# Two-layer cross-attention on one NeuronCore: the softmax factors 1/l of layer 0 taken to the features by a VectorE transpose and a trip through DRAM, in place of TensorE transposes

## The chip, the cores and the metric

The kernel runs on one NeuronCore of a Trainium2 chip. The metric is device time in microseconds (us) of one execution; lower is better. The engines named below are TensorE (PE, with its weight loads as PEld), VectorE (DVE), ScalarE (ACT), GpSimd (POOL) and SyncE (SP, which only issues DMAs here).

## What is computed

Four batches of 1024 query rows of 512 features pass through two cross-attention layers, each with a residual. Everything is float32. The change lies in layer 0:

```python
# layer 0: 16 heads of 64, 1024 queries, 1024 keys
h = layernorm(x) * gamma + beta
Q = (h @ Wq).reshape(B, NQ, 16, 64)
K = (context @ Wk).reshape(B, NC, 16, 64)
V = (context @ Wv).reshape(B, NC, 16, 64)
attn = softmax(einsum("bihd,bjhd->bhij", Q, K), axis=-1) * 64 ** -0.5
x = x + einsum("bhij,bjhd->bihd", attn, V).reshape(B, NQ, 1024) @ Wo + bo
# layer 1: RMS norm, 16 heads of 32, rotary embedding, q and k of unit length
x = x + attention1(x, context) @ wout
```

The softmax divides by a row sum l, one for each query and head. The kernel multiplies by 1/l after the product with V, where the queries lie along the free dimension and the 128 partitions are the features of two heads. So each 1/l, which is made with queries on partitions, has to be turned and repeated over the 64 features of its head.

## The kernel before, in words

The 16 heads of layer 0 are done as 8 pairs (`p`), and the 1024 queries of a pair as 8 tiles of 128 (`i`). One call of `Attention0.step` (L381 and on) does one tile for both heads. Two steps, an even one and an odd one, make a block (`BQ = 2`); there are 32 blocks in a batch and 128 in all. A step runs so:

- `scores`: TensorE makes the scores of the two heads, 8 matmuls (L372).
- VectorE takes the row maximum (L393), and ScalarE the exponentials with their row sums, into `e` and `l` (L394), once for each head.
- Filler work on TensorE, taken from the list `work` by `Units.fill`: projections of the next pairs, output projection of earlier ones, in pieces with a cost in us, spread by a planner over the steps that are left.
- VectorE transposes `e` in 32x32 blocks (L399). After the odd step, 16 DMAs from SP's queue (L406) put these blocks in the order that a matmul wants, into `eT`: 128 KB and 128 runs of 1 KB each.
- VectorE takes the reciprocal of the sums (L410). In an even step with two blocks in hand, `product` multiplies the older one's `eT` by V (L451, 32 matmuls, "AV" from here on) and scales by the factors (L458). So AV of a block comes more than one step after its `eT` DMAs are issued.

The factors go a way of their own. In the even step, `factors` lets GpSimd spread the 4 sums' reciprocals of the block over 256 columns times 64 ** -0.5 (L424). At the top of the next even step, `factors_turned` has TensorE transpose them, two transposes of 128x128 (L442), right behind the scores; ScalarE copies the result from PSUM to the place where `vals` will stand (L443); and VectorE multiplies AV by that copy (L458).

What sets the order: the engines run their instructions in program order (`manual_schedule`), SP's queue holds the `eT` DMAs, the pairs' weights (L313), the rows of x (L287), and the stores. ScalarE's queue issues DMAs only at the very start. The framework gives every DMA, of SP's queue or of ScalarE's, one of eight completion semaphores in turn, in the order in which its scheduler wrote the program, and lets a DMA wait until the DMA eight places before it has landed. In the order written for this kernel, the even step's second exponential is over after the second or third `eT` DMA of the block before it (103 of 127 blocks), and the odd step's after the eighth or ninth (99 of 127).

Buffers: `e` has two, so that the exponentials of a block wait for the `eT` DMAs of the block two before. Four PSUM banks (`bank`) are used in turn by filler, transposes and AV.

Of the kernel before, what the change touches and what calls it, by code (L numbers as in the profile page):

```python
# [30 lines left out]
F32 = mybir.dt.float32  # L31
AF = mybir.ActivationFunctionType
ALU = mybir.AluOpType
AX = mybir.AxisListType

P = 128
# [7 lines left out]
HD0 = 64  # L44
# [63 lines left out]
def xattn_kernel(ctx: ExitStack, tc: tile.TileContext, a: dict, out: bass.AP):  # L108
    nc = tc.nc
# [3 lines left out]
    const = ctx.enter_context(tc.tile_pool(name="const", bufs=1))  # L113
    sb = ctx.enter_context(tc.tile_pool(name="sb", bufs=2))
    ps_s = ctx.enter_context(tc.tile_pool(name="ps_s", bufs=2, space=bass.MemoryType.PSUM))
    ps_f = ctx.enter_context(tc.tile_pool(name="ps_f", bufs=1, space=bass.MemoryType.PSUM))
    ctx.enter_context(tc.manual_schedule())

    def score(name, shape=(P, S)):
# [4 lines left out]
    def bank(name):  # L124

        which["n"] = which["n"] + 1 if which["n"] < 3 else which["from"]
        return ps_f.tile([P, 512], F32, tag=f"f{which['n']}", name=name)
# [5 lines left out]
    ident = const.tile([P, P], F32, name="ident")  # L133
# [2 lines left out]
    nc.gpsimd.memset(ones, 1.0)  # L136
    nhalf = const.tile([P, 16], F32, name="nhalf")
    nc.gpsimd.memset(nhalf, -0.5)
    cols = const.tile([P, 3, NQ], F32, name="cols")
    bo = const.tile([P, DQ], F32, name="bo")  # L140
    cos = const.tile([P, NT, HD1], F32, name="cos")
# [27 lines left out]
    def flush():  # L169
        while posts:  # L170
            posts.pop(0)()
# [120 lines left out]
    def add_units(xt, lhs, w, name, cs, then=None):  # L292

        n = len(cs)

        def one(t, i, pp=[None]):
            if i == 0:
                pp[0] = bank(f"{name}_{t}")
            matmul(pp[0], lhs(cs[i])[:, t * P : (t + 1) * P], w(cs[i]), i == 0, i == n - 1)
            if i == n - 1:  # L300
                nc.vector.tensor_add(xt[t], xt[t], pp[0])  # L301
                if then is not None:
                    then(t)

        return [[(0.86, lambda t=t, i=i: one(t, i)) for i in range(n)] for t in range(NT)]
# [51 lines left out]
    BQ = 2  # L357
    r = [slice(j * HD0, (j + 1) * HD0) for j in range(2)]

    class Attention0:  # L360
# [20 lines left out]
        def step(self, p, i, pr, us):  # L381
            n = f"{self.b}_{p}_{i}"
            sc = self.scores(p, i, pr)
            if i % BQ == 0 and len(self.blocks) == 2:
                self.factors_turned()
            m = sb.tile([P, 2], F32, tag="m", bufs=3, name=f"m_{n}")
            l = sb.tile([P, 2], F32, tag="l", bufs=3, name=f"l_{n}")
            if i % BQ == 0:
                self.e = sb.tile([P, BQ, 2, S], F32, tag="e", bufs=2, name=f"e0_{n}")
                self.li = sb.tile([P, BQ, 2], F32, tag="li", bufs=4, name=f"li_{n}")  # L390
            e = [self.e[:, i % BQ, j, :] for j in range(2)]
            for j in range(2):
                nc.vector.tensor_reduce(m[:, j : j + 1], sc[j], AX.X, ALU.max, negate=True)  # L393
                nc.scalar.activation(e[j], sc[j], AF.Exp, bias=m[:, j : j + 1], accum_out=l[:, j : j + 1])  # L394
            holds["posts"] = True
            self.u.fill(min(us, 1.8))
            holds["posts"] = False
            for j in range(2):
                nc.vector.transpose(e[j], e[j])  # L399
            flush()  # L400
            if i % BQ == BQ - 1:
                eT = sb.tile([P, 2 * BQ, 4, S // 4], F32, tag="big", bufs=2, name=f"eT_{n}")
                of = self.e.rearrange("p t h s -> p (t h) s")
                for g in range(4):
                    for q in range(4):
                        nc.sync.dma_start(  # L406
                            eT[32 * g : 32 * (g + 1), :, q, :],
                            of[32 * q : 32 * (q + 1), :, g * (S // 4) : (g + 1) * (S // 4)],
                        )
            nc.vector.reciprocal(self.li[:, i % BQ, :], l)  # L410
            if i % BQ == BQ - 1:
                eT = eT.rearrange("p (t h) a s -> p h t a s", h=2)
                self.blocks.append((p, i // BQ, pr, eT, self.li))
            elif self.blocks:
                if len(self.blocks) == 2:
                    self.product()
                self.factors()
            self.u.fill(us - min(us, 1.8))

        def factors(self):  # L420

            li = self.blocks[0][4]
            self.rb = sb.tile([P, BQ, P], F32, tag="rb", bufs=2, name=f"rb_{self.blocks[0][:2]}")
            nc.gpsimd.tensor_scalar(  # L424
                self.rb.rearrange("p t (j d) -> p (t j) d", j=2),
                li.rearrange("p t j -> p (t j)").unsqueeze(2).to_broadcast([P, 2 * BQ, HD0]),
                HD0**-0.5,
                0.0,
                ALU.mult,
                ALU.add,  # L430
            )

        def factors_turned(self):

            p, q, pr = self.blocks[0][:3]
            W = BQ * P
            if q == 0:
                pr["vals"] = sb.tile([P, S], F32, tag="vals", bufs=4, name=f"vals0_{self.b}_{p}")
            self.o = pr["vals"][:, q * W : (q + 1) * W]
            rT = bank(f"rT_{self.b}_{p}_{q}")  # L440
            for k in range(BQ):
                nc.tensor.transpose(rT[:, k * P : (k + 1) * P], self.rb[:, k, :], ident)  # L442
            nc.scalar.copy(self.o, rT[:, :W])  # L443

        def product(self):
            p, q, pr, eT, _ = self.blocks.popleft()
            o, W = self.o, BQ * P
            av = bank(f"av_{self.b}_{p}_{q}")
            for k in range(NT):
                for j in range(2):  # L450
                    nc.tensor.matmul(  # L451
                        av[r[j], :W].rearrange("p (t a i) -> p t a i", t=BQ, a=4),
                        pr["v"][:, k, r[j]],
                        eT[:, j, :, :, k * 32 : (k + 1) * 32],
                        start=k == 0,
                        stop=k == NT - 1,
                    )
            nc.vector.tensor_mul(o, av[:, :W], o)  # L458


    TH = 2
# [206 lines left out]
    def flat(lists):  # L668
        return [u for lst in lists for u in lst]
# [54 lines left out]
    work = Units()  # L724
# [7 lines left out]
    AV = 3.9  # L732
# [8 lines left out]
    for b in range(B):  # L741
        ct, hT, pairs = st["ct"], st["hT"], st["pairs"]
        xt = []
        att = Attention0(b, work)
# [3 lines left out]
        for p in range(NPAIR):  # L748
# [15 lines left out]
            elif p % 2 == 0:  # L764
                i = p // 2 - 1
                wo[i] = wo_load(a["Wo"], i, f"wo0_{b}_{i}")
                outs = add_units(
                    xt,
                    lambda n: pairs[n]["vals"],
                    lambda n, i=i: wo[i][:, n % 2, :],  # L770
                    f"po0_{b}_{i}",
                    (p - 2, p - 1),
                )
# [3 lines left out]
            if p == 6:  # L777
                kT, qT = qk_tile(f"k1_{b}_0"), qk_tile(f"q1_{b}_0")
                k = rotated_chains(kT, ct, NC_, lambda k, wk=wk: wk[:, k, :], f"k1_{b}_0", RowScratch())
                other = k[0][0] + outs[0] + k[1][0] + outs[1] + k[0][2] + outs[2] + k[2][0] + k[1][2] + outs[3]  # L780
            if p == NPAIR - 1:
                last = outs[4:]
                wo[3] = wo_load(a["Wo"], 3, f"wo0_{b}_3")
                outs = add_units(
                    xt, lambda n: pairs[n]["vals"], lambda n: wo[3][:, n % 2, :], f"po0_{b}_3", (6, 7)
                )
                xnT = []
                norms = norm_units(b, 1, xnT, lambda h: xt[4 * h : 4 * h + 4])
# [11 lines left out]
            for i in range(NT):  # L800
# [8 lines left out]
                n = NT * (NPAIR - p if later else 1) - i  # L809
# [15 lines left out]
        q = rotated_chains(qT, xnT, NQ, lambda k, wq=wq: wq[0][:, k, :], f"q1_{b}_0", tmp)  # L825
        k1 = rotated_chains(kT1, ct, NC_, lambda k, wk1=wk1: wk1[0][:, k, :], f"k1_{b}_1", tmp)
        q1 = rotated_chains(qT1, xnT, NQ, lambda k: wq1[:, k, :], f"q1_{b}_1", tmp)

        def second():
            att.product()  # L830
            att.factors()

        att.factors_turned()
        work.add([(AV, second)] + flat(outs[:4]) + norms[0]["stats"])
        work.add(k1[0][0] + [(0.2, att.factors_turned)] + norms[0]["apply"] + [(AV, att.product)])
        work.add(norms[0]["turn"] + q[0][0] + k1[1][0] + k1[0][2] + flat(outs[4:]) + q[0][2])
        work.drain()

# [2 lines left out]
        o = [  # L841
            sb.tile([P, S], F32, tag="vals", bufs=4, name=f"o1_{b}_{g}") if g < 2 else None
            for g in range(4)
        ]
# [6 lines left out]
        for half in range(2):  # L851
            n = 0
# [51 lines left out]
        else:  # L904
            outs = add_units(
                xt, lambda n, o=o: o[n], lambda n, w=wo1[1]: w[:, n % 2, :], f"po1_{b}_1", (2, 3), store
            )
# [39 lines left out]
```

## Time and profile before

| | |
|---|---|
| median of 3 runs | 2992.65 us (2991.08 to 2992.93) |
| the profiled execution: its time, its span | 2989.95 us, 2987.7 us |
| PE busy | 2917.3 us, 98% of the span |
| DVE busy | 2230.7 us, 75% |
| ACT busy | 1429.5 us, 48% |
| POOL busy | 416.6 us, 14% |
| DMA engines, mean share in layer 0 (four stretches of 460 to 480 us) | 0.72 to 0.73 |
| DMA engines, mean share in layer 1 | 0.03 to 0.09 |

Durations come from the one profiled execution, whose span runs from the first to the last instruction. TensorE's granted clock is 0.996 of full speed over the whole. Matmuls are pipelined, so a matmul's own duration is longer than its distance to the next; the times below that say what a matmul costs are distances from start to start. A wait is put down to what ended it last by the profile. Times in a timeline are us from the span's start.

### The profile page before, as it was taken

How to read it: one execution, taken by the hardware profiler on the slowest of the kernel's cores; microseconds unless marked ns; L12 is line 12 of the kernel's file. 1: busy time of each engine (PE TensorE's matmuls, PEld its weight loads, DVE VectorE, ACT ScalarE, POOL GpSimd, SP SyncE). 2: the span in 40 equal slices, each digit the busy share in tenths (PEclk: the TensorE clock that was granted, in tenths of full speed). 3: DMA queues.
4: the chain of work that ended last, by engine and by line, in shares of the span. 5: the costliest groups of instructions: out<-in, count | busy, mean ns of one | idle time of the engine just before them, and what ended most of it. 6: DMA issues, size and time to landing. Idle time of an engine off the chain costs nothing.

```text
span 2987.7 us, 60793 instructions
## 1 busy us (share of the span) xinstructions
PE 2917.3 (98%) x24748; PEld 1544.2 (52%) x24748; DVE 2230.7 (75%) x2824; ACT 1429.5 (48%) x2265; POOL 416.6 (14%) x392
## 2 busy tenths in 40 slices
PE   8999999999999999999999999999999999999998
PEld 5544546555544555655554454555455445455544
DVE  4777795877777779587777777958777777795777
ACT  3444443666443444465644344446664444444664
POOL 0010022420000002232000000223200000022310
PEclk9999999999999999999999999999999999999999
DMA  5788674010387867301048776730104978772000
GB/s 148 169 192 180 158 178 112 22 35 25 81 203 185 186 163 171 94 21 35 25 98 207 175 183 166 171 84 21 35 25 113 205 176 182 170 169 69 2 2 30
DMA packets 374134, 348.50 MB, mean 117 GB/s; under 512 B 37600, under 2 KB 355296, under 8 KB 373856
## 3 DMA queue, kind: packets, MB, share of 16 engines
q1 hardware_dynamic: 371664, 343.43, 48.4%
q8 instruction: 197, 3.23, 0.5%
q10 hardware_dynamic: 2192, 1.19, 0.2%
q14 instruction: 81, 0.66, 0.1%
HBM read 67.64 MB, written 8.39 MB: 25 GB/s over the span
## 4 chain that ended last, share of the span: by engine, by line
PE 78%; DVE 10%; DMA 4%; SPq 3%; ACT 2%; issue 1%; POOL 1%; DVEq 0%; ACTq 0%
PE s L372 14%; PE av L451 13%; PE po L158 10%; PE pv L158 7%; PE s L599 7%; PE av L638 6%; PE pqT L158 6%; PE pkT L158 5%; PE q_p L158 3%; DMA eT<-e 2%; SPq L406 2%; PE av L649 2%; DVE both L615 2%; DVE e L399 2%; PE k_p L158 1%; DVE m L393 1%
## 5 line engine op out<-in xcount | busy, mean ns | idle before, releaser
L394 ACT ACTIVATE e<-s,m 128x1024 f32<-128x1024 f32 x512 | 565.6, 1109 | 679.2 <-DVE m L393 613.8
L393 DVE TENSOR_REDUCE m<-s 128x1 f32<-128x1024 f32 x512 | 602.8, 1219 | 320.0 <-PE s L372 320.0
L399 DVE STREAM_TRANSPOSE e<-e 128x1024 f32<-128x1024 f32 x512 | 606.7, 1224 | 54.9 <-ACT e L394 43.0
L609 ACT ACTIVATE e<-s 128x1024 f32<-128x1024 f32 x512 | 496.5, 1022 | 315.1 <-PE s L599 300.1
L372 PE MATMUL s<-qk 64*128 64x512 f32 x2048 | 520.5, 615 | 6.0 <-ACT e L394 5.3
L451 PE MATMUL av<-eT,v 128*64 128x256 f32 x4096 | 474.8, 385 | 15.6 <-DMA eT<-e 13.7
L615 DVE TENSOR_TENSOR both<-e 128x512 f32<-128x512 f32 x512 | 342.4, 701 | 127.7 <-ACT e L609 92.5
L451 PEld LDWEIGHTS av<-eT,v 128*64 128x64 f32 x4096 | 289.4, 138 | 214.0 <-issue 53.7
L372 PEld LDWEIGHTS s<-qk 64*128 64x128 f32 x2048 | 181.8, 186 | 262.6 <-issue 188.9
L599 PE MATMUL s<-q,k 32*128 32x256 f32 x4096 | 305.7, 402 | 5.8 <-ACT q L526 2.7
L599 PEld LDWEIGHTS s<-q,k 32*128 32x128 f32 x4096 | 191.6, 185 | 149.7 <-ACT e L609 71.4
L158 PE MATMUL po<-wo,vals 128*128 128x512 f32 x512 | 239.6, 601 | 2.5 <-ACT v L130 2.5
L158 PE MATMUL pqT<-hT,w 128*128 128x512 f32 (+1 forms) x800 | 241.3, 597 | 0.7 <-ACT hT L255 0.7
L443 ACT COPY vals<-rT 128x256 f32<-128x256 f32 x128 | 47.7, 372 | 327.4 <-PE rT L442 327.4
L301 DVE TENSOR_TENSOR x<-x,po 128x512 f32<-128x512 f32 x200 | 133.8, 679 | 82.8 <-PE po L158 82.8
L158 PEld LDWEIGHTS pv<-w,cT 128*128 128x128 f32 (+1 forms) x2400 | 176.7, 152 | 30.3 <-issue 27.2
L158 PE MATMUL pv<-w,cT 128*128 128x128 f32 (+1 forms) x2400 | 186.5, 275 | 0.0
L158 PE MATMUL pkT<-cT,w 128*128 128x512 f32 (+1 forms) x600 | 181.6, 599 | 1.1 <-ACT cT L130 1.1
L619 DVE TENSOR_TENSOR both<-both 128x1024 f32<-128x1024 f32 x128 | 159.7, 1248 | 4.4
L158 PEld LDWEIGHTS po<-wo,vals 128*128 128x128 f32 x512 | 90.9, 190 | 106.4 <-issue 101.4
L158 PEld LDWEIGHTS pqT<-hT,w 128*128 128x128 f32 (+1 forms) x800 | 85.9, 151 | 112.2 <-issue 105.9
L638 PE MATMUL av<-e,v 128*32 128x256 f32 x2048 | 137.0, 385 | 0.0
(461 smaller groups left out, 2667.0 us busy)
## 6 DMA issues: line engine op xcount, KB each, us to landing
eT<-e SPq DMA_DIRECT2D x2048, 128.0 KB, 2.8
xr<-in_x_dram SPq DMA_DIRECT2D x32, 256.0 KB, 4.3
x<-in_x_dram SPq DMA_DIRECT2D x32, 256.0 KB, 3.8
wo<-in_Wo_dram SPq DMA_DIRECT2D x16, 512.0 KB, 4.2
out_dram<-x SPq DMA_DIRECT2D x32, 256.0 KB, 2.7
w<-in_Wq_dram SPq DMA_DIRECT2D x31, 256.0 KB, 4.0
c<-in_ctx_dram SPq DMA_DIRECT2D x32, 192.0 KB, 4.5
wkv<-in_wkv_dram SPq DMA_DIRECT2D x16, 384.0 KB, 3.5
```

The lines of the kernel that those rows point to most:

```text
L158: nc.tensor.matmul(o[rr], lhsT[:, rr], rhs, start=start, stop=stop)
L301: nc.vector.tensor_add(xt[t], xt[t], pp[0])
L372: nc.tensor.matmul(sc[j][:, kb * 512 : (kb + 1) * 512], pr["qT"][r[j], i * P : (i + 1) * P], pr["kT"][r[j], kb * 512 : (kb + 1) * 512], st ...
L393: nc.vector.tensor_reduce(m[:, j : j + 1], sc[j], AX.X, ALU.max, negate=True)
L394: nc.scalar.activation(e[j], sc[j], AF.Exp, bias=m[:, j : j + 1], accum_out=l[:, j : j + 1])
L399: nc.vector.transpose(e[j], e[j])
L451: nc.tensor.matmul(av[r[j], :W].rearrange("p (t a i) -> p t a i", t=BQ, a=4), pr["v"][:, k, r[j]], eT[:, j, :, :, k * 32 : (k + 1) * 32], ...
L599: nc.tensor.matmul(sc[j // 2][:, j % 2, c, :], kT[rr, g, k * P : (k + 1) * P], qT[rr, g, qb * WQ : (qb + 1) * WQ], start=True, stop=True,)
L609: nc.scalar.activation(e, sc[u], AF.Exp, scale=float(np.sqrt(np.float32(HD1))))
L615: nc.vector.tensor_add(self.both[:, kk, 2 * u : 2 * u + 2, :], es[u][:, :, 0, :], es[u][:, :, 1, :])
L619: nc.vector.tensor_add(self.both[:, 0], self.both[:, 0], self.both[:, kk])
L638: nc.tensor.matmul(self.av[rr, 0, :], v[g][:, 2 * kk + c, rr], es[j // 2][:, j % 2, c, :], start=first and c == 0, stop=end and c == 1,)
```

## The change

The reciprocals of a block are taken at once, after its odd step, into the first 4 columns of a 128x32 tile `sums` that is otherwise one. VectorE transposes that tile in 32x32 blocks into `turned`, so that the 128 queries of factor k lie on the 4 partitions k, k+32, k+64, k+96. In the next (even) step, behind the exponentials, ScalarE's queue issues 4 DMAs, one for each factor, of 4 runs of 128 B, to a DRAM tile `rows` (`factors_out`). In the odd step, again behind the exponentials, it issues 2 DMAs, one for each head, that read 256 numbers from DRAM back onto 64 partitions each, into `fac` (`factors_back`); they wait for the 4 to have landed. `product` then multiplies AV by 64 ** -0.5 and by `fac` in one VectorE instruction. The transposes, the PSUM bank they took, ScalarE's copy and GpSimd's spreading are gone. At the end of a batch the same calls stand in the list of work.

```diff
+    dram = ctx.enter_context(tc.tile_pool(name="dram", bufs=3, space=bass.MemoryType.DRAM))
+    sums = const.tile([P, 32], F32, name="sums")
+    nc.gpsimd.memset(sums, 1.0)
...
         def step(self, p, i, pr, us):
             sc = self.scores(p, i, pr)
-            if i % BQ == 0 and len(self.blocks) == 2:
-                self.factors_turned()
...
-                nc.scalar.activation(e[j], sc[j], AF.Exp, bias=m[:, j : j + 1], accum_out=l[:, j : j + 1])
+                l = self.l[:, i % BQ, j : j + 1]
+                nc.scalar.activation(e[j], sc[j], AF.Exp, bias=m[:, j : j + 1], accum_out=l)
+            if self.blocks:
+                (self.factors_back if i % BQ else self.factors_out)()
...
-            nc.vector.reciprocal(self.li[:, i % BQ, :], l)
-            if i % BQ == BQ - 1:
+                self.factors(n)
...
-            elif self.blocks:
-                if len(self.blocks) == 2:
-                    self.product()
-                self.factors()
+            elif len(self.blocks) == 2:
+                self.product()
+        def factors(self, n):
+            nc.vector.reciprocal(sums[:, : 2 * BQ].rearrange("p (j t) -> p t j", j=2), self.l)
+            turned = sb.tile([P, 32], F32, tag="li", bufs=1, name=f"li_{n}")
+            nc.vector.transpose(turned, sums)
+            self.turned = turned
+
+        def factors_out(self):
+            block = self.blocks[-1]
+            rows = dram.tile([2 * BQ, 4, 32], F32, tag="rows", name=f"rows_{block[0]}_{block[1]}")
+            for k in range(2 * BQ):
+                nc.scalar.dma_start(rows[k], self.turned[k : k + 97 : 32, :])
+            block[4] = rows.rearrange("(j t) a i -> j (t a i)", j=2)
+
+        def factors_back(self):
+            block = self.blocks[-1]
+            fac = sb.tile([P, BQ * P], F32, tag="rb", bufs=2, name=f"fac_{block[0]}_{block[1]}")
+            for j in range(2):
+                nc.scalar.dma_start(fac[r[j]], block[4][j].partition_broadcast(HD0))
+            block[4] = fac
...
-            rT = bank(f"rT_{self.b}_{p}_{q}")
-            for k in range(BQ):
-                nc.tensor.transpose(rT[:, k * P : (k + 1) * P], self.rb[:, k, :], ident)
-            nc.scalar.copy(self.o, rT[:, :W])
...
-            nc.vector.tensor_mul(o, av[:, :W], o)
+            nc.vector.scalar_tensor_tensor(o, av[:, :W], HD0**-0.5, fac, ALU.mult, ALU.mult)
...
-        att.factors_turned()
-        work.add([(AV, second)] + flat(outs[:4]) + norms[0]["stats"])
-        work.add(k1[0][0] + [(0.2, att.factors_turned)] + norms[0]["apply"] + [(AV, att.product)])
+        att.factors_out()
+        work.add([(AV, att.product)] + flat(outs[:4]) + norms[0]["stats"])
+        work.add(k1[0][0] + [(0.0, att.factors_back)] + norms[0]["apply"] + [(AV, att.product)])
```

More of the change, by code (lines that the diff above doesn't have):

```diff
@@ L383, in step @@
             sc = self.scores(p, i, pr)
-            if i % BQ == 0 and len(self.blocks) == 2:
-                self.factors_turned()
             m = sb.tile([P, 2], F32, tag="m", bufs=3, name=f"m_{n}")
-            l = sb.tile([P, 2], F32, tag="l", bufs=3, name=f"l_{n}")
             if i % BQ == 0:
                 self.e = sb.tile([P, BQ, 2, S], F32, tag="e", bufs=2, name=f"e0_{n}")
-                self.li = sb.tile([P, BQ, 2], F32, tag="li", bufs=4, name=f"li_{n}")
+                self.l = sb.tile([P, BQ, 2], F32, tag="l", bufs=2, name=f"l_{n}")
             e = [self.e[:, i % BQ, j, :] for j in range(2)]
@@ L409, in step, with product @@
                         )
-            nc.vector.reciprocal(self.li[:, i % BQ, :], l)
-            if i % BQ == BQ - 1:
+                self.factors(n)
                 eT = eT.rearrange("p (t h) a s -> p h t a s", h=2)
-                self.blocks.append((p, i // BQ, pr, eT, self.li))
-            elif self.blocks:
-                if len(self.blocks) == 2:
-                    self.product()
-                self.factors()
-            self.u.fill(us - min(us, 1.8))
[L420 to L435, printed above, removed]
+                self.blocks.append([p, i // BQ, pr, eT, None])
+            elif len(self.blocks) == 2:
+                self.product()
+            self.u.fill(us - min(us, 1.8))
+        def factors(self, n):
[15 more added lines that the diff above has]
+            block[4] = fac
+        def product(self):
+            p, q, pr, eT, fac = self.blocks.popleft()
             W = BQ * P
@@ L438, in factors_turned @@
                 pr["vals"] = sb.tile([P, S], F32, tag="vals", bufs=4, name=f"vals0_{self.b}_{p}")
-            self.o = pr["vals"][:, q * W : (q + 1) * W]
-            rT = bank(f"rT_{self.b}_{p}_{q}")
-            for k in range(BQ):
-                nc.tensor.transpose(rT[:, k * P : (k + 1) * P], self.rb[:, k, :], ident)
-            nc.scalar.copy(self.o, rT[:, :W])
-        def product(self):
-            p, q, pr, eT, _ = self.blocks.popleft()
-            o, W = self.o, BQ * P
+            o = pr["vals"][:, q * W : (q + 1) * W]
             av = bank(f"av_{self.b}_{p}_{q}")
@@ L827, in xattn_kernel @@
         q1 = rotated_chains(qT1, xnT, NQ, lambda k: wq1[:, k, :], f"q1_{b}_1", tmp)
-        def second():
-            att.product()
-            att.factors()
-        att.factors_turned()
-        work.add([(AV, second)] + flat(outs[:4]) + norms[0]["stats"])
-        work.add(k1[0][0] + [(0.2, att.factors_turned)] + norms[0]["apply"] + [(AV, att.product)])
+        att.factors_out()
+        work.add([(AV, att.product)] + flat(outs[:4]) + norms[0]["stats"])
+        work.add(k1[0][0] + [(0.0, att.factors_back)] + norms[0]["apply"] + [(AV, att.product)])
         work.add(norms[0]["turn"] + q[0][0] + k1[1][0] + k1[0][2] + flat(outs[4:]) + q[0][2])
```

## The prediction

> **What bounds the kernel now.** First the page: the busy shares, then the chain that ended last.
>
> ```profile
> PE 2917.3 (98%) x24748; PEld 1544.2 (52%) x24748; DVE 2230.7 (75%) x2824; ACT 1429.5 (48%) x2265; POOL 416.6 (14%) x392
> ...
> PE 78%; DVE 10%; DMA 4%; SPq 3%; ACT 2%; issue 1%; POOL 1%; DVEq 0%; ACTq 0%
> ```
>
> TensorE carries 78% of the chain, so work taken from it in layer 0 counts in full as long as nothing else comes due; but DMA and SP's queue together hold 7%, so a second limit is near. Second, the timeline around one block (columns: start, us, engine, line, what).
>
> ```profile
> 1019.55 1.95 SPq L406 DMA_DIRECT2D eT<-e  x3
> ...
> 1023.38 11.07 SPq L406 DMA_DIRECT2D eT<-e  x13
> ...
> 1024.61 0.44 PE L442 MATMUL rT<-ident,rb_(4, 0)_7884 128*128 128x128 f32 x2
> ...
> 1024.89 1.02 PE L158 MATMUL pqT<-hT,w 128*128 128x512 f32 x2
> ...
> 1026.05 3.67 PE L451 MATMUL av<-eT,v 128*64 128x256 f32 x32
> ```
>
> From the first transpose (1024.61) to the next matmul (1024.89) TensorE spends 0.28 us. Over all 128 pairs in the trace this distance has a mean of 0.287 us. SP's queue is issuing `eT` DMAs almost all the time; those that end at 1021.50 belong to the block whose AV starts at 1026.05. Third, that transfer and its waiters, from the view of tile `eT` (ns min/median/max; then who waited, us and times), and SP's own waits (us, times, longest).
>
> ```profile
> L406 SPq DMA_DIRECT2D eT<-e x2048: 585/601/2250, 42.4 to 2708.0; - x187
> ...
>   ACT e L394: 56.2, 63
> ...
> DMA to landing us min/median/max: 2.4/2.8/9.2
> ```
>
> ```profile
> SPq L406 <- DVE li L410: 315.5, 99, 26.5
> ```
>
> The exponentials wait 63 times for an `eT` transfer, and SP is idle before `eT` for only 315.5 us, 2.5 us a block. I then laid the trace out by blocks. Times from the end of a block's last transpose on VectorE (call it d), medians over the 122 blocks with all their followers in the same batch: first `eT` DMA issued at +0.1, the 16 issued in 10.75, the last landed at +13.2; the following even step's second exponential starts at +4.3, the odd step's at +11.15; the next d comes at +13.7; AV starts at +16.6. What AV has in hand after the landing, over all 128 blocks: median 3.1 us, lower quartile 2.0, and under 0.5 in 11 blocks, those with pair weights or rows in SP's queue. The `eT` transfer, not TensorE alone, is what the change must not delay.
>
> Fourth, the one place where both queues issue DMAs, the start, with two landings from the DMA view (last column, us).
>
> ```profile
> 0.72 0.47 ACTq L313 DMA_DIRECT2D w<-in_Wk_dram  x1
> ...
> 0.72 1.82 SPq L188 DMA_DIRECT2D c<-in_ctx_dram  x4
> ...
> 2.31 0.51 ACTq L146 DMA_DIRECT2D cols<-in_gamma_dram  x1
> 3.58 0.35 ACTq L146 DMA_DIRECT2D cols<-in_beta_dram  x1
> ...
> 4.15 4.47 SPq L279 DMA_DIRECT2D xr<-in_x_dram  x4
> ...
> 5.57 0.33 ACTq L146 DMA_DIRECT2D cols<-in_norm_w_dram  x1
> ```
>
> ```profile
> w<-in_Wq_dram ACTq DMA_DIRECT2D x1, 256.0 KB, 4.3
> ...
> w<-in_Wk_dram ACTq DMA_DIRECT2D x1, 192.0 KB, 3.4
> ```
>
> Eight DMAs go out at once, four from each queue. SP's fifth starts at 4.15, when ScalarE's first has landed (0.72 + 3.4 = 4.12), and ScalarE's sixth at 5.57, when its second has (1.21 + 4.3 = 5.51). That is the ring of eight semaphores: a DMA of one queue can hold up the other queue.
>
> **What the Trainium skill says.** "DMA: Bandwidth & Descriptors", section "Why a DMA increments its semaphore by 16 and not by 1": two transfers in flight on one semaphore can't be told apart, so each wants its own; the start above agrees, since a semaphore is reused only after a landing. The same page, "Two DMAs through the same engine are not ordered": a read of what a DMA wrote must wait for that DMA's semaphore, so the two read-backs can't follow the four writes blindly; no DMA of this trace does this. "Perfetto Trace Analysis", section "DMA Instruction — HWDGE (DVE, Sync)": the descriptor generator is locked by one sequencer at a time, and a DMA's row leaves out the movement of data. The trace shows no cost of the lock: SP's four at the start took 0.455 us each beside ScalarE's, and four row loads alone later 0.44 each (1.75 us, at 12.56).
>
> **The change part by part.**
>
> *TensorE.* 128 pairs of transposes go: 128 x 0.287 = 36.7 us, all on the main path (TensorE is busy 463.66 of 470 us in a stretch of layer 0). One PSUM bank less in the turn can only ease waits; I take nothing.
>
> *ScalarE.* 128 copies of 0.372 us go. Six DMA issues a block come. ScalarE's nine issues at the start took 0.33 to 0.53 us; at 0.45 that is 2.7 us a block. ScalarE is busy 190.74 of 470 us there, 5.6 us of a 13.7 us block, so 8 us are free. The issues stand behind the second exponential, which runs 1.1 us; the trace has ScalarE's semaphore waits going on while an earlier activation still runs, so the sequencer can issue meanwhile. Behind them are queued the evacuations of filler banks, and TensorE waits for those only after three more banks. Cost nothing, hidden by that idle time; if the sequencer couldn't run ahead, the DMAs would start 1.3 us later (below).
>
> *VectorE.* Two reciprocals of 0.125 us go; one of 128x4 (at most 0.15) and a transpose of 128x32 come. The 128x1024 transpose takes 1.224 us, so between 0.04 and 0.2. The three-operand product is not in the trace; the nearest row is the product it replaces, 0.409 us, from PSUM too; bounds 0.35 to 0.6. Sum between -0.1 and +0.2 us a block; I take zero, since VectorE is idle a quarter of the block. GpSimd's 0.404 us of spreading goes; nobody is short of it.
>
> *DMA traffic.* 16 + 128 packets a block beside 2048 of `eT`: 7% of packets at a share of 0.72, so 0.77. Taken as nothing; bound +0.3 us on the landing.
>
> *The factors themselves.* Rows are written at d + 4.4 and landed 2 to 3 us later; read back at d + 11.2; landed by d + 14; needed when AV ends, d + 20. Six us to spare. `turned`, with one buffer, is free by d + 8.5 and written again at d + 13.7. At a batch's end (4 times) the read-back has the statistics of the norm and the projections ahead of AV as its cover.
>
> *The ring.* This is the part that costs. The four writes and two reads take places among the 16 `eT` DMAs. By the order of the kernel before, the first write comes after the third `eT`, and the eighth place after it is the eighth `eT`. That one now waits for the write's landing. Issue and landing of a write: 0.4 us, and 2.0 to 2.3 behind it (`eT` 2.8 with 0.6 of issue; a 256 KB store 2.7 with 0.38); I take 2.4, range 2.0 to 3.4. So the eighth `eT` goes at 4.35 + 2.4 = d + 6.75, where it went at 0.1 + 7 x 0.65 = 4.65: 2.1 late, and the sixteenth at 6.75 + 8 x 0.65 = 11.95 instead of 9.85. The first read comes after the ninth `eT`, and the eighth place after it is the sixteenth: it waits until 11.2 + 2.4 = 13.6. It lands 2.8 later, at d + 16.4, where it landed at 13.2: 3.2 late. AV asks 0.29 earlier, so the delay that counts is 3.5.
>
> What that costs by block: the part of 3.5 us that the block's time in hand doesn't cover, less what the block before has already stood still (its `eT` gained that). Over the 128 values this sums to 73 us (115 without that credit). The same sum for delays of 1, 2, 2.5, 3, 4 and 5 us gives 9, 27, 40, 55, 97 and 153. The exponentials two blocks on wait for the same landing, at the same moment as AV, and add nothing of their own.
>
> Sum: 2989.95 - 36.7 + 73 = 3026 for a profiled execution; the median of the runs lies 2.7 above the profiled one, so 3028.
>
> **The rivals.**
>
> *The ring's places fall kindly (faster).* If the scheduler writes the DMAs of ScalarE one or two `eT` later, the first write holds only the tenth `eT` (delay under 1 us) and the first read holds the next block's first, which waits for VectorE anyway. For: the places are mine by inference, and one step of 0.65 us decides for the read. Against: two thirds of blocks have the odd step's exponential at eight or nine, not ten. Delay 1 to 2: 2992.65 - 36.7 + 9 to 27 = 2965 to 2983. It decides below a delay of about 2.4 us, where the cost is 36.7.
>
> *ScalarE or the generator becomes the bound (much slower).* If ScalarE issues only after the exponential has run (+1.3), or each of the six locks out SP for 0.4 us (2.4 us on a queue with 2.5 idle), the delay is 5 or more: 2992.65 - 36.7 + 153 = 3109. For: the lock of the skill's page. Against: 0.455 beside 0.44 us.
>
> *In between.* Delay 2.2 to 2.7: 2987 to 3001, no change to speak of. That TensorE's 36.7 us don't come off is hardly possible; the instructions are gone.
>
> **How the numbers follow.** Ring delays of 3 to 4.5 us 0.49 (3011 to 3080); kind places 0.24; ScalarE or generator 0.18; in between 0.09. The likeliest gives 3028. The range is 2964 to 3112: it takes in the kind case whole and the worst case's lower half. Its own range for the likeliest is 3008 to 3080. A measurement of this kernel can tell about 0.2% (6 us) from no change. Faster by more: the kind places and a little of the in-between, 0.26; within: 0.07; slower: 0.67.
>
> **What would show it.** Right: no L442 or L443; a gap in SP's `eT` issues about seven in and another before the last one, with SP waiting on a DMA of `rows` or `fac`; the 16 taking some 14 us from first to last; AV and the exponentials waiting for `eT` well over the 13.7 and 56.2 us of before; TensorE's busy time down by some 40 us and its idle time up by more. Wrong: `eT` issued in 10.75 us as before and TensorE's idle time unchanged (then about 2956 to 2965), or ScalarE's DMA rows near 1 us each, or the product waiting for `fac`.

## The result, and the profile after

The changed kernel takes 3150.14 us, median of 4 runs (3140.84 to 3153.6), beside 2991.86 us for the kernel before on the same chip: a ratio of 1.052, 95% interval 1.0501 to 1.0539. It is slower, as forecast, but by 158 us where the forecast said 36. The profiled execution took 3153.09 us, with a span of 3151.3.

The page after, busy shares, the chain that ended last, and the group of AV's matmuls (busy us, mean ns | idle us before it and what ended most of it):

```profile
PE 2941.3 (93%) x24492; PEld 1577.9 (50%) x24492; DVE 2256.8 (72%) x2824; ACT 1400.2 (44%) x2137; POOL 366.2 (12%) x265
...
PE 64%; DMA 14%; DVE 9%; SPq 6%; ACT 3%; issue 2%; POOL 1%; ACTq 0%; DVEq 0%
...
L451 PE MATMUL av<-eT,v 128*64 128x256 f32 x4096 | 520.9, 411 | 158.4 <-DMA eT<-e 103.0
```

AV's group on the page of the kernel before:

```profile
L451 PE MATMUL av<-eT,v 128*64 128x256 f32 x4096 | 474.8, 385 | 15.6 <-DMA eT<-e 13.7
```

TensorE lost 256 transposes and is busy longer than before. Its part of the chain fell from 78% to 64%, and DMA and SP's queue went from 7% to 20%. In front of AV it stands idle for 158.4 us (15.6 before), and one AV matmul takes 411 ns on average (385 before).

Next, SP's own waits in the changed kernel (us, times, longest us):

```profile
SPq L409 <- DMA fac<-rows: 256.0, 154, 5.4
...
SPq L409 <- DMA rows<-li: 59.5, 73, 2.7
...
SPq L409 <- DVE li L424: 26.9, 2, 26.7
```

Before, SP waited 315.5 us for VectorE ahead of `eT`: it had time to spare and stood ready when a block was finished. Now nearly all of that time goes to landings of the two factor transfers, which no `eT` DMA needs. The view of tile `eT` shows who waits in turn:

```profile
L409 SPq DMA_DIRECT2D eT<-e x2048: 585/601/2230, 42.3 to 2867.1; - x187
...
  ACT e L395: 233.3, 50
```

The issue of one `eT` DMA is unchanged at 601 ns. Last, the timeline over one block in the middle of a batch (start, us, engine, line, what, idle before and what ended it):

```profile
1021.51 1.14 ACTq L439 DMA_DIRECT2D fac<-rows  x2
...
1025.34 1.12 PE L161 MATMUL pqT<-hT,w 128*128 128x512 f32 x2
...
1029.11 1.11 ACT L395 ACTIVATE e<-s,m 128x1024 f32<-128x1024 f32 x1 [5.83 <-DMA eT<-e]
1029.20 3.67 PE L451 MATMUL av<-eT,v 128*64 128x256 f32 x32 [2.73 <-DMA eT<-e]
```

The reads go out at 1021.51. AV and the exponential, which need the last `eT` of the block, start together more than seven us later, after a pause of TensorE of 2.73 us.

**Where the time went.** The span grew by 163.6 us. TensorE's idle time went from 66.7 to 206.3 us (+139.6). The trace's record of the granted clock has 146.8 us of the span at half speed instead of 24.4. TensorE stood idle for 26.9 us of these (1.7 before); half of what is left, 59.9 instead of 11.4 us, is work lost to the slow clock (+48.6 from the unrounded figures). That leaves -24.6 us for all else, and the transposes are what TensorE no longer does. In each of the eight changed kernels of the table the same sum leaves between -23.3 and -25.6 us. So the transposes gave some 24 us in every one of them, and not the 36.7 that the prediction took off (more on this at the end).

By place, with "layer 0" from a batch's first scores to the last block's end "batch end" from there to layer 1's first scores, and "layer 1" from these to its last scores, sums over four batches, in us ("after" is the changed kernel; of each figure in the last column some 2 us lie behind the last instruction):

| kernel | span | layer 0 | batch ends | layer 1 | TensorE idle | at half clock |
|---|---|---|---|---|---|---|
| before | 2987.7 | 1773.9 | 142.1 | 1014.1 | 66.7 | 26.9 |
| after | 3151.3 | 1904.8 | 174.7 | 1014.6 | 206.3 | 148.7 |
| `no_dma` | 2970.8 | 1762.1 | 141.5 | 1010.1 | 68.4 | 41.2 |
| `wr_only` | 3037.1 | 1792.9 | 172.0 | 1014.9 | 114.6 | 88.8 |
| `rd_only` | 3110.1 | 1883.0 | 154.5 | 1014.5 | 174.6 | 119.6 |
| `pool` | 3014.7 | 1771.4 | 173.4 | 1012.9 | 97.5 | 81.9 |
| `early` | 3555.2 | 2310.0 | 173.4 | 1014.8 | 455.2 | 511.3 |
| `end_pool` | 3127.2 | 1897.0 | 158.9 | 1015.0 | 187.4 | 125.8 |
| `pool_back` | 2970.1 | 1762.4 | 141.5 | 1009.1 | 76.7 | 23.1 |

Two things stand out for the changed kernel: layer 0's blocks lost 131 us, and the four batch ends lost 33 us, which the prediction had costed at nothing.

**The ring, seen DMA by DMA.** The trace tells which of the eight semaphores each DMA of the two queues raised, and when. For every `eT` DMA I took the DMA before it on the same semaphore. Of the 202 that follow a read-back, none starts before that read has landed, 158 start after a pause of SP of over 0.15 us, and 122 of these start within 60 ns of the landing, at a median of 17 ns behind it. Those 122 pauses sum to 238 us. For the writes it is 72 pauses and 60 us. So an `eT` DMA starts the moment a factor transfer that it has nothing to do with lands. Of the pauses for a read, 73 stand before the 16th `eT` of a block and 37 before the 15th; of those for a write, 63 stand before the 7th to 10th.

### The profile page after: what moved, and what is told of

It is laid out like the page before. It is cut to its first block, busy times and chain, and to the rows that moved or that the text cites. A ratio compares the mean times of both kernels' runs of the same rounds, so it can differ in the third digit from the quotient of the medians.

```text
span 3151.3 us, 60534 instructions
## 1 busy us (share of the span) xinstructions
PE 2941.3 (93%) x24492; PEld 1577.9 (50%) x24492; DVE 2256.8 (72%) x2824; ACT 1400.2 (44%) x2137; POOL 366.2 (12%) x265
## 4 chain that ended last, share of the span: by engine, by line
PE 64%; DMA 14%; DVE 9%; SPq 6%; ACT 3%; issue 2%; POOL 1%; ACTq 0%; DVEq 0%
PE av L451 13%; PE s L375 10%; PE s L599 7%; PE po L161 7%; PE pv L161 6%; PE av L638 6%; DMA eT<-e 6%; SPq L409 5%; DMA fac<-rows 5%; PE pqT L161 4%; PE pkT L161 3%; PE q_p L161 3%; DVE m L393 3%; PE av L649 2%; ACT e L395 2%
## 5 line engine op out<-in xcount | busy, mean ns | idle before, releaser
L402 DVE STREAM_TRANSPOSE e<-e 128x1024 f32<-128x1024 f32 x512 | 607.0, 1224 | 142.1 <-ACT e L395 70.2
L451 PE MATMUL av<-eT,v 128*64 128x256 f32 x4096 | 520.9, 411 | 158.4 <-DMA eT<-e 103.0
L451 PEld LDWEIGHTS av<-eT,v 128*64 128x64 f32 x4096 | 346.1, 148 | 361.5 <-issue 201.0
L293 POOL TENSOR_TENSOR x<-x,bo 128x512 f32<-128x512 f32 x32 | 40.8, 1275 | 932.1 <-DMA x<-in_x_dram 488.8
```

The source lines that it names most:

```text
L451: nc.tensor.matmul(av[r[j], :W].rearrange("p (t a i) -> p t a i", t=BQ, a=4), pr["v"][:, k, r[j]], eT[:, j, :, :, k * 32 : (k + 1) * 32], ...
```

## The experiments

Two theories stood at the start. **The ring**: the cost is the wait for a semaphore that a factor DMA still holds, and which factor DMA holds which `eT`. **Lock or traffic**: the cost is the issue of six more DMAs (ScalarE's time, or the descriptor generator) or the bytes and packets that they move. Later a third was tested, that the factors simply arrive late.

**`pool`: the same six DMAs from GpSimd's queue**, which takes its semaphores elsewhere than SP's and ScalarE's ring: in the trace its DMAs raise semaphores 111 to 118, where those of SP and ScalarE share 100 to 107.

```diff
-                nc.scalar.dma_start(rows[k], self.turned[k : k + 97 : 32, :])
+                nc.gpsimd.dma_start(rows[k], self.turned[k : k + 97 : 32, :])
-                nc.scalar.dma_start(fac[r[j]], block[4][j].partition_broadcast(HD0))
+                nc.gpsimd.dma_start(fac[r[j]], block[4][j].partition_broadcast(HD0))
```

> The changed kernel with its six factor DMAs of a block issued from GpSimd's queue instead of ScalarE's; same bytes, same places in the program. Theory (ring): GpSimd's DMAs have semaphores of their own, so no eT DMA waits for rows or fac; the 16 eT are issued in about 11 us again, nothing waits for eT beyond the 70 us of before, and only the saving on TensorE is left: 2955 to 2970 us. Rival (traffic or the descriptor generator: the added packets or issues slow eT): the same packets are there, so 3100 to 3150. Rival (ScalarE held up by its own issues): 2955 to 2970 too, but then eT's issue would have taken 11 us in the changed kernel as well, which it didn't.

Measured: 3018.03 us (3016.45 to 3022.66), ratio to before 1.0099 (1.0067 to 1.0132). Of the 158 us, 132 are gone with the transfers still there, and layer 0 is at 1771.4 us, below the kernel before. The move changes more than the semaphores. On GpSimd's queue the DMAs do not stand behind the exponentials: the first write goes out at d + 0.6 and the first read at d + 5.4 (4.4 and 11.4 in after; medians, d being a block's end), and ScalarE issues nothing. `pool` alone doesn't part the ring from ScalarE's issues, then; SP's waits above do, since they end as factor DMAs land. With both, the 132 us are the ring's share. But the value is far over the 2955 to 2970 that I expected, and the table shows where: the batch ends still take 173.4 us. There it is not the ring. `pool`'s timeline at a batch end, and below it TensorE's waits:

```profile
491.27 1.05 POOL L512 TENSOR_TENSOR rot<-rot,k_r 128x512 f32<-128x512 f32 x1
492.27 1.18 POOL L439 DMA_DIRECT2D fac<-rows  x2
495.57 0.42 DVE L458 SCALAR_TENSOR_TENSOR vals<-av,fac 128x256 f32<-128x256 f32 x1 [6.36 <-DMA fac<-rows]
496.05 1.12 PE L256 MATMUL pth<-ident,xn 128*128 128x128 f32 x4 [5.58 <-DVE vals L458]
```

```profile
PE pth L256 <- DVE vals L458: 22.1, 4, 5.6
```

The batch's last two reads stand on GpSimd behind the keys' power (2.98 us) and multiplication, because the work list names `k1[0][0]` ahead of them. AV is done at 487.9, its factors land at 495.5, and the next transposes want the PSUM bank that AV still holds. So `pool` mends one hold and opens another.

**`no_dma`, `wr_only`, `rd_only`: parts alone.** All three multiply by ones, so the factors 1/l are left out of the output; the ones come from a constant tile in `no_dma` and `wr_only`, and from DRAM in `rd_only`. `no_dma` has neither writes nor reads, `wr_only` has the four writes of each block and no reads, and `rd_only` has the two reads of each block from a DRAM tile written once.

```diff
+    fixed = const.tile([P, 256], F32, name="fixed")
+    nc.gpsimd.memset(fixed, 1.0)
...
-            block[4] = fac
+            block[4] = fixed
```

In `rd_only` instead:

```diff
+    rows1 = dram.tile([4, 4, 32], F32, tag="rows1", bufs=1, name="rows1")
+    for k in range(4):
+        nc.gpsimd.dma_start(rows1[k], sums[k : k + 97 : 32, :])
+    back1 = rows1.rearrange("(j t) a i -> j (t a i)", j=2)
...
+            block[4] = back1
```

> The changed kernel without the six factor DMAs: the product uses a fixed tile of ones instead of the factors read back, so the factors are left out of the result. Everything else stays (reciprocals, VectorE's transpose, the product in one instruction). Theory: the floor of the change, TensorE's 36.7 us and nothing else: 2950 to 2960 us. If it stays above 2980, something other than the DMAs costs.

> The changed kernel with the four writes a block and without the two reads: the product uses a fixed tile of ones, so the factors are left out. Theory (ring): the eighth eT is still held until the first write has landed, some 2.2 us, and the sixteenth no more; last eT issued at d + 12 instead of 14.1; 2990 to 3030 us. Rival (lock of the descriptor generator, cost by issue): four sixths of the 195 us: 3085. Rival (traffic): 2 KB a block are nothing: 2955.

> The changed kernel with the two reads a block and without the four writes: the reads take a DRAM tile that is written once at the start, so the factors are constant and wrong. Theory (ring): the sixteenth eT is held until the first read has landed, at d + 13.9 to 14.1 as in the changed kernel, whatever the writes do; 3080 to 3140 us. Rival (lock, by issue): two sixths of 195 us: 3020. Rival (traffic): nearly all bytes are in the reads: 3140.

Measured: `no_dma` 2969.13 us, ratio 0.9927 (0.9904 to 0.995); `wr_only` 3037.13, ratio 1.0158 (1.0116 to 1.02); `rd_only` 3111.59, ratio 1.0407 (1.0365 to 1.0449). The order is that of the ring and not of the lock: two reads cost 142 us over `no_dma` and four writes only 68. Of the writes' 68 us nearly half lies at the batch ends (172.0 us against 141.5), which the expectation hadn't counted. Traffic alone doesn't give it either, since `pool` moves all of it and its layer 0 loses 9 us to `no_dma`. `rd_only` fell in the middle of what the ring was to give and `wr_only` 7 us over its upper end. Together they exceed the 181 us of the whole, probably because a block held by its read has partly been held by its write already. And `no_dma`, which is all that the change could bring, saves 20 us and not 36.7 (more on this at the end).

**`early`: the writes issued four us sooner.** The reads move too, from the odd step to the next even one (d + 5.7 instead of 11.4). This is what one would try if the factors came late.

```diff
-            if self.blocks:
-                (self.factors_back if i % BQ else self.factors_out)()
+            if self.blocks and i % BQ == 0:
+                self.factors_back()
...
                 self.blocks.append([p, i // BQ, pr, eT, None])
+                self.factors_out()
...
-        att.factors_out()
```

> After with the four writes issued right behind VectorE's turn, four us sooner than in after, and the reads behind the next even step's exponentials. If what costs is that the factors come late, this is faster than after: 3000 to 3100. If what costs is the ring of eight, this is much slower than after: the writes now stand in the written order among the last quarter transfers of the block before, and hold them until they have landed, some 2.8 us into the next block. The last landing then comes 4 us later than the values product wants it, in nearly every block, and the product runs at half clock after the pause: 4 to 6.5 us on 128 blocks, 3500 to 3800 (over 3300 in any case).

Measured: 3553.43 us (two runs, 3549.84 and 3557.01), ratio 1.1879 (1.1858 to 1.1899). The chain and AV's group on its page, and the first of SP's waits:

```profile
PE 53%; DVE 19%; DMA 15%; issue 4%; ACT 4%; SPq 3%; POOL 1%; ACTq 0%; DVEq 0%
...
L452 PE MATMUL av<-eT,v 128*64 128x256 f32 x4096 | 673.9, 501 | 411.6 <-DMA eT<-e 297.3
```

```profile
SPq L409 <- DMA rows<-li: 608.2, 125, 7.7
```

The transfers are the same and their data are ready sooner, yet the kernel is 400 us slower than after. The held DMAs are now the 14th (32 times) and 15th (66 times) `eT` of a block, and they wait for the writes of the block after it. The place in the written order decides, and lateness of the factors is out as the cause.

**`end_pool`: the batch ends alone.** The six DMAs of a batch's last block go from GpSimd, and its reads stand before the statistics; all else is as in after.

```diff
-        def factors_out(self):
+        def factors_out(self, queue=nc.scalar):
...
-        def factors_back(self):
+        def factors_back(self, queue=nc.scalar):
...
-        att.factors_out()
-        work.add([(AV, att.product)] + flat(outs[:4]) + norms[0]["stats"])
-        work.add(k1[0][0] + [(0.0, att.factors_back)] + norms[0]["apply"] + [(AV, att.product)])
+        att.factors_out(nc.gpsimd)
+        work.add([(AV, att.product)] + flat(outs[:4]) + [(0.0, lambda: att.factors_back(nc.gpsimd))] + norms[0]["stats"])
+        work.add(k1[0][0] + norms[0]["apply"] + [(AV, att.product)])
```

> After, but the six factor transfers of a batch's last block alone go from GpSimd's queue, and its two reads are issued before the statistics instead of behind the keys' chain. If the 8 us that after loses in each batch behind its last block come from the ring (the last five quarter transfers of block 30 wait for the reads' landing and one for a write's), this gives 4 x 8.2 = 33 us back: 3117 (3110 to 3128). If they come from the lateness of the factors themselves or from the work list's new order, it stays within 8 us of after: 3142 to 3158.

Measured: 3134.01 us (3126.4 to 3143.97), ratio 1.0479 (1.0458 to 1.05): 16 us better than after, half of the 33. The batch ends fell from 174.7 to 158.9, not to 142. The trace says why. The timeline of the changed kernel at the first batch end, where the last block is finished at 507.73:

```profile
505.31 1.14 ACTq L439 DMA_DIRECT2D fac<-rows  x2
...
508.70 0.52 ACTq L431 DMA_DIRECT2D rows<-li  x1
...
514.54 6.20 PE L451 MATMUL av<-eT,v 128*64 128x256 f32 x32 [5.94 <-DMA eT<-e]
```

This AV belongs to block 30. The same instruction in the kernel before, whose block 31 was finished at 475.88:

```profile
476.84 3.67 PE L451 MATMUL av<-eT,v 128*64 128x256 f32 x32
```

In after, the 12th `eT` of block 30 goes at 508.49, 10 ns after the second of these reads landed (508.48), and the 15th at 510.99, 20 ns after the first of these writes landed (510.97). The 16th lands at 514.1, AV comes 5.94 us late, and it runs at half clock for 6.20 us where it took 3.67. `end_pool` took the write out of the ring, but the reads are block 30's and I had left them on ScalarE. In `end_pool` the 16th goes at 0.9 to 1.2 us behind block 31's end (3.8 to 3.9 in after), and AV still waits 2.7 to 3.2 us. What is left, 4.2 us a batch, is that hold. So the batch ends are the ring too, and my expectation missed one of its two holds.

**`pool_back`: all on GpSimd, the last reads moved.** Against `pool`:

```diff
-        work.add([(AV, att.product)] + flat(outs[:4]) + norms[0]["stats"])
-        work.add(k1[0][0] + [(0.0, att.factors_back)] + norms[0]["apply"] + [(AV, att.product)])
+        work.add([(AV, att.product)] + flat(outs[:4]) + [(0.0, att.factors_back)] + norms[0]["stats"])
+        work.add(k1[0][0] + norms[0]["apply"] + [(AV, att.product)])
```

> The version with all six factor transfers on GpSimd's queue, its last reads of a batch issued before the statistics. In the version without this move the last product of a batch waited 5.6 us for two reads that stood on GpSimd behind a 3 us power and a multiplication, and with the slow clock after it that was 8 us a batch. If that is the cause, 31 us come back from 3018: 2987 (2980 to 2994), level with the kernel before or a little faster. If the 8 us a batch have another cause, 3010 to 3022.

Measured: 2986.69 us, median of 14 runs (2971.85 to 2994.52), ratio 0.9981 (0.9971 to 0.9991), so 31 us below `pool` and a little below the kernel before. (`pool` ran on another chip. Beside the kernel before on its own chip, `pool` lies 28.5 us over it and `pool_back` 4.8 us under it.) TensorE's busy time and AV's group:

```profile
PE 2889.6 (97%) x24492; PEld 1526.0 (51%) x24492; DVE 2252.4 (76%) x2824; ACT 1387.1 (47%) x2137; POOL 800.7 (27%) x1033
...
L451 PE MATMUL av<-eT,v 128*64 128x256 f32 x4096 | 475.4, 385 | 28.1 <-DMA eT<-e 20.6
```

The batch ends are at 141.5 us, as in `no_dma`, and AV's mean is 385 ns again. The profiled execution is the fastest of the 14, so its table row shows the good end. The runs' mean clocks lie between 0.989 and 0.996, and the longer runs have the lower clocks. It lies 0.2% under the kernel before, about as little as can be told from no change.

## Why the prediction was right and where it was wrong

**The price of the ring was the wrong term.** The prediction charged 73 us for the ring and took off 36.7 for the transposes. The traces have 188.2 us (139.6 of idle time, 48.6 of slow clock) and 24.6. Of the idle time, pauses ahead of AV grew by 23.1 us at the four batch ends and by 119.7 in all other blocks (from 15.6 to 135.3); TensorE's other idle time fell by 3.2. The steps that made the price too low follow.

**The mechanism was right, and in half of the blocks so were most of its times.** In the 60 blocks without other loads ahead of their `eT` in SP's queue (batch ends aside, medians from a block's end d): first write issued at 4.42 and landed at 6.68, where the prediction had 4.35 and 6.75; first read issued at 11.44 and landed at 14.16 (11.2 and 13.6); last `eT` landed at 16.63 (16.4). In these blocks it had landed at 12.73 before, though, and not at the 13.2 of all blocks, so that the delay is 3.9 us and not 3.2. A read takes 2.74 us from issue to landing and a write 2.32; I had 2.4 for both. The lock rival is out: `eT` issues take 601 ns as before, though ScalarE's own take 0.52 and not 0.45 us.

**The step "less what the block before has already stood still" was wrong.** It credited each block with the pause of the block before, on the ground that SP's queue gains it. But the held DMAs are SP's own. In those same blocks the last `eT` is issued at d + 14.14 and takes 0.6, while the next block ends at d + 13.85: the queue is late when the next block is ready. The first `eT` of a block starts at d + 1.31 instead of d + 0.06. The delay is carried over, not credited. Without the credit the prediction had 115 us, near the 119.7 found; in part that is luck, since the delays weren't the 3.5 us of that sum either.

**One order for all blocks was assumed.** In the other 60 blocks, with pair weights, rows of x or stores ahead of their `eT`, the first `eT` starts at d + 2.39, the last is landed at d + 18.7 (13.68 before), and AV starts at d + 19.06 (16.87). The delay there is 5 us and not 3.2, and among these are the blocks that had the least in hand. The first sort lost 50.1 us of period in sum and the second 80.8; both are net of what the transposes gave.

**"Cover" at the batch end was the wrong question.** I asked whether the factors of the last block come in time. They do. But block 30's AV follows at once, without the scores of a next block, so the ring's hold on block 30's last `eT` has nothing to hide behind: 5.5 to 5.9 us of wait and some 2.5 us of slow clock, four times, 33 us.

**The clock was not in the sum at all.** "TensorE: Matmul & The Clock Gate" of the Trainium skill, section "What's actually happening", states that TensorE's clock falls to half after an idle window of about 3.4 us, and that the windows run free of the kernel. The trace agrees in the length: its slow stretches last 3.41 or 6.83 us. But a pause of TensorE need not be that long. Of the changed kernel's 98 AVs behind a pause under 2 us none ran slow; of the 24 behind a pause over 2.5 us, 22 did, among them 3 of the 4 whose pause was under 3 us. From the first matmul's start to the last one's, an AV behind 2.5 to 3 us of pause took 4.83 us on average, and 5.45 behind longer ones, where 3.30 is usual. The 48.6 us of slow clock come on top of the idle time, and my 73 were idle time alone.

**TensorE's 36.7 us were mis-sized: the gain is 24.** I took the distance from the first transpose to the matmul behind the pair, and overlooked that this next matmul changes too. The first matmul behind the scores starts 0.52 us after the last score's start in any case; before it was a transpose, now it is a projection. A projection with 512 columns that stands there takes 0.53 us to its successor, and one behind the transposes took 0.43. The lines above show it: two `pqT` take 1.02 us in the kernel before (at 1024.89, in the prediction) and 1.12 in the changed one (at 1025.34). In the kernel before, the steps without transposes have the 0.53 as well. So a pair saves 0.19 us on average (`pool_back`, the 117 pairs with the same neighbours and no pause), and 128 of them save 24 us. Why the first matmul behind the scores takes longer was not tried. In `no_dma`, whose span is 16.9 us shorter than before, these 24.4 us of work stand against 7.5 more of idle time and slow clock.

**Traffic** was put at 0 with a bound of 0.3 us on the landing. In `pool`, without the ring's hold, the last landing is 0.85 us later than before. It is hidden in most blocks: in layer 0 TensorE is idle for 32.7 us in `pool` and 32.6 in `pool_back`, where `no_dma` has 25.5, so the traffic costs some 7 us. The rest of the 9 us between `pool` and `no_dma` in the table is slow clock.

Of the rivals, the kind places can be set aside: the places fell as inferred. The 3109 us of the slow rival came nearest in size, for a reason that wasn't its own.

## What to carry to other kernels

A DMA added on one queue can stop another queue that shares its completion semaphores: write down the order in which the program assigns them, find the DMA eight places behind each new one, and compare its usual start with the new one's landing. When that moves a transfer on which the kernel's pace depends, ask what comes due at the next block and at the end of a stage, where the usual cover is missing, and add the clock that TensorE loses after a pause of some 2 us or more (in `early`, 6 of the 10 AVs behind 2 to 2.5 us of pause ran slow). A queue with a ring of its own (here GpSimd's) removes the coupling, but then every instruction ahead on that engine is a wait for the DMA.

## What had not been expected

Issuing the same small writes four us sooner, and the reads with them, cost 400 us (`early`). The transposes were not worth their distance from start to start, 0.287 us a pair, but 0.19: the matmul that moved into its place took 0.1 us longer. A pause of TensorE doubles as a tax on the work behind it: an AV of 3.67 us took 6.20 after 5.94 us of waiting, and in `early` 216 of 3555 us were lost to the clock ((509.3 us at half speed - 77.3 of them idle) / 2). Four DMAs of 512 bytes each take 2.32 us to land, nearly as long as a read-back of 64 KB (2.74), so their size said nothing about how long they hold a semaphore.
